# A gated cross-attention block on one core: the first fetch of x, the late weights and the weight rounding moved

## The chip, the cores and the metric

The kernel runs on one core of a Trainium2 chip. The metric is the device time of one execution in microseconds (us). The engines are TensorE (PE; PEld is its weight load), VectorE (DVE), ScalarE (ACT), GpSimd (POOL) and SyncE (SP, which here only issues DMAs).

## The reference

Sixteen sequences x of 224 tokens by 512 attend to contexts of 750 keys by 384 with 8 heads; a mask drops some keys of each sequence. A feed-forward part with quantised activations and ternary weights follows. Both parts are gated and added to x:

```
x = x + tanh(g_xattn) * xattn(layernorm(x), context, mask)
x = x + tanh(g_ffn)   * ffn(layernorm(x))

xattn: softmax(mask(q k^T / 8)) v W_o + b_o,  q = x W_q, k = context W_k, v = context W_v
ffn:   bitlinear(gelu(bitlinear(h, w1, b1)), w2, b2)
bitlinear(h, w, b): h is rms-normalised and quantised to 8 bits by row;
                    scale = 1 / max(mean|w|, 1e-5); w = clip(round(w * scale), -1, 1) / scale
```

w1 is 2048 by 512, w2 is 512 by 2048. All inputs and the output are float32, except the mask.

## The kernel before, in words

**Opening.** `order_batches` (L30) reads the mask, counts the keys that each sequence keeps, and sorts the sequences by that count into 16 slots. The first 8 slots hold up to 192 keys and the others up to 128. It leaves tables in SBUF: `sh.slots` (per slot its number of keys and its sequence), `sh.upto` (running counts of kept keys) and `sh.token` (row numbers of x). At its end `n_odd` goes to every engine's register (L150), and the program branches (L226): `compact_path` (L709) if all slots fit, which is what runs here, otherwise `dense_path`.

**Start of the compact path.** POOL first writes two ramps, `place` and `place_f` (L785 to L790), scales the sequence numbers to row offsets (`first`, L792) and zeroes two buffers `v_rest` (L851). Then:

- `fetch(i)` (L915) gathers two 128-token tiles of x by indirect DMA, which POOL issues. Three buffers of two tiles rotate.
- `select(s)` (L797) makes the list of kept keys of slot s. Six compares on DVE make `ind` (L803), PE sums it (L810), DVE makes `keys` (L819) and the mask (L826).
- `gather(s)` (L831) fetches the kept rows of the context by indirect DMA.
- `norm(i)` (L921) is the layernorm of x. DVE takes the statistics (L929, L930). POOL makes the power -1/2 (L761) and subtracts and multiplies (L938).
- `query_pieces` (L963) turns x on PE (L951) and multiplies by W_q (L972). `context_pieces` (L854) turns the context (L867) and makes keys (L876) and values (L891).

**Slots.** `scores` (L1001) makes the logits on PE (L1011), the row maxima on DVE (L1025), the exponentials on ACT (L1035), the reciprocal on DVE (L1044) and the product on POOL (L1045). `turn_probs` transposes the result (L1065, L1072) and `weighted` multiplies it by the values (L1089, L1100). While slot s runs, the context and queries of slot s+1 and the statistics of s+2 are prepared.

**Weights.** `load_weights` (L1299) loads w1 or w2 in eight blocks of 512 KB through SP. `sum_weights` (L1314) adds up magnitudes, even blocks on DVE (L1321), odd ones on ACT (L1325). `scale_weights` (L1329) makes the total over partitions with a matmul (L1333) and the scale on DVE (L1335 to L1344). `round_weights` (L1350) scales, clips and casts a block on DVE (L1354, L1355, L1356) into one of two rotating buffers `w16` with tag `xq`. `turn_weights` (L1359) transposes that on PE (L1367, L1371) and an evictor writes it as 8-bit floats. w1 is prepared within slot 0 and w2 within slot 1. `late_loads` (L220) fetches b_o, b2, W_o and b1; POOL scales b_o and b2 by the gates (L1454, L1455).

**Feed-forward part.** From slot 2 on, pairs of 128-token tiles go through `residual` (fetches of y, L1139, and the addition of b_o, L1141), `project` (L1143), `normalise` (L1172), `up` (L1209), `gelu` (L1231) and `down` (L1260). `normalise` uses two buffers with tag `xq`: `xq`, and `xqT`, a DMA transpose of it (L1196).

**What sets the order.** The lists at L1418 to L1482 are merged by hand-given costs (`merge`, L1389), which gives the order in which the program is written. A scheduler below then orders each engine's instructions by readiness and priority, so that the order on an engine is not the order of the source. [...] `evict` (L738) chooses DVE or ACT for PSUM evictions by a running balance of estimated loads.

Of the kernel before, what the change touches and what calls it, by code (L numbers as in the profile page):

```python
# [16 lines left out]
EPS = 1e-5  # L17
# [12 lines left out]
def order_batches(ctx, tc, sh, mask, x, context):  # L30
# [33 lines left out]
    def spread(dst, src, first, second):  # L64
# [8 lines left out]
        second.tensor_copy(dst[32:64, :, 5:6], by4[32:64, :, 3:4])  # L73
        second.tensor_copy(dst[64:128, :, 5:6], by4[64:128, :, 3:4])

    spread(spread_no, start, nc.gpsimd, nc.gpsimd)
    nc.gpsimd.tensor_tensor(at, at, spread_no, ALU.add)
    tri = sel.tile([TJ, TJ], BF16, name="tri")
# [11 lines left out]
    kept = sel.tile([B, 1], F32, name="kept_of")  # L90
    nc.vector.tensor_reduce(kept, m8, AX.X, ALU.add)
    nc.gpsimd.tensor_copy(m, m8)

    key = sel.tile([B, 1], F32, name="key")
    nc.vector.scalar_tensor_tensor(key, kept, float(B), number, ALU.mult, ALU.add)
# [39 lines left out]
    nc.vector.tensor_reduce(odds, odd, AX.XY, ALU.add)  # L135
    n_odd = const.tile([1, 1], mybir.dt.int32, name="n_odd")
    nc.vector.tensor_copy(n_odd, odds)

    where = sel.tile([P, 4, 8], F32, name="where")
    spread(where, sh.slots[:, 1, :], nc.vector, nc.gpsimd)  # L140
# [568 lines left out]
def compact_path(ctx, tc, sh, x, context, out, late_loads):  # L709
# [53 lines left out]
    def small(name, n=2):  # L763
        return pa.tile([P, n], F32, tag=f"s{n}", name=name, bufs=24 if n == 2 else 6)
# [16 lines left out]
        )  # L781

    place = pa.tile([P, 256], BF16, name="place")  # L785
    numbers(place[:, :192], [[1, 192]], 0, 0)
    numbers(place[:, 192:], [[1, 64]], 128, 0)
    place_f = pa.tile([TQ, 320], BF16, name="place_f")
    numbers(place_f[:, :192], [[1, 192]], 0, 0)
    numbers(place_f[:, 192:], [[1, P]], 0, 0)  # L790
    first = pa.tile([P, B], F32, name="first")
    nc.gpsimd.tensor_scalar(first, sh.slots[:, 1, :], float(J), None, ALU.mult)  # L792

    live = [{} for _ in range(B + 1)]
    kctx = context.rearrange("b j c -> (b j) c")

    def select(s):  # L797

        st = live[s]
        nt = 2 if CAPS[s] > P else 1  # L800
        ind = pa.tile([TJ, NJ, 256], BF16, tag="ind", name=f"ind_{s}", bufs=1)
        for n in range(NJ):
            nc.vector.tensor_scalar(  # L803
                ind[:, n, : nt * P], place[:TJ, : nt * P], sh.upto[:, n, s : s + 1], None, ALU.is_ge
            )
# [12 lines left out]
        keys = pa.tile([P, 2], I32, tag="keys", name=f"keys_{s}", bufs=3)  # L818
        nc.vector.tensor_scalar(  # L819
            keys[:, :nt], pi[:, :nt], float(J - 1), first[:, s : s + 1], ALU.min, ALU.add  # L820
        )
# [4 lines left out]
        nc.vector.tensor_scalar(  # L826
            mb[:, :nm], place_f[:, :nm], sh.slots[:TQ, 0, s : s + 1], -FMAX, ALU.is_ge, ALU.mult
        )
        st["mask"] = mb

# [17 lines left out]
    v_rest = []  # L848
    for i in range(2):
        t = pa.tile([P, NP, 2, DH], F32, name=f"v_rest_{i}")  # L850
        nc.gpsimd.memset(t, 0.0)  # L851
        v_rest.append(t)

    def context_pieces(s):  # L854
# [66 lines left out]
    def norm(i, ks=(0, 1)):  # L921

        xp = normed[i]
        name = f"x{i}_{ks[0]}"
        part = slice(ks[0], ks[-1] + 1)
        mv = small(f"mv_{name}", 4).rearrange("p (k n) -> p k n", k=2)
        for k in ks:
            st = small(f"bs_{name}_{k}", 6)
            nc.vector.bn_stats(st, xp[:, k, :])  # L929
            nc.vector.bn_aggr(mv[:, k, :], st)  # L930
            load["v"] += 850
        rstd = small(f"rs_{name}")
        nc.gpsimd.tensor_scalar(rstd[:, part], mv[:, part, 1], 1.0, EPS, ALU.mult, ALU.add)
        pow_half(rstd[:, part])
        less = small(f"ls_{name}")
        nc.gpsimd.tensor_scalar(less[:, part], mv[:, part, 0], -1.0, 0.0, ALU.mult, ALU.add)
        for k in ks:
            nc.gpsimd.tensor_scalar(  # L938
                xp[:, k, :], xp[:, k, :], less[:, k : k + 1], rstd[:, k : k + 1], ALU.add, ALU.mult
            )  # L940

    def slot_xnT(s):
        if "xnT" not in live[s]:
# [228 lines left out]
    def normalise(i, ks=(0, 1)):  # L1172
# [126 lines left out]
    def load_weights(wi, c):  # L1299

        raws[wi, c] = raw = late["raw"].tile([P, W], F32, tag="raw", name=f"raw_{wi}_{c}", bufs=NPC)
        if wi == 0 and c == 0:

            nc.scalar.copy(raw[0:1, 0:1], live[0]["ctx"][0:1, 0, 0:1])
        if wi == 0:
            nc.sync.dma_start(
                raw.rearrange("p (a d) -> p a d", d=D),
                sh.w1_dram[c * 2 * P : (c + 1) * 2 * P, :].rearrange("(a p) d -> p a d", p=P),
            )
        else:  # L1310
            at = c % 2 * W
            nc.sync.dma_start(raw, sh.w2_dram[c // 2 * P : (c // 2 + 1) * P, at : at + W])

    def sum_weights(wi, c):  # L1314
        if c == 0:
# [34 lines left out]
    def round_weights(wi, c):  # L1350

        raw = raws.pop((wi, c))
        quantised[wi, c] = w16 = pa.tile([P, W], BF16, tag="xq", name=f"w16_{wi}_{c}", bufs=2)
        nc.vector.tensor_scalar(raw, raw, weight_scale[wi], 1.0, ALU.mult, ALU.min)  # L1354
        nc.vector.tensor_scalar(w16.bitcast(I16), raw, -1.0, None, ALU.max)  # L1355
        nc.vector.tensor_copy(w16, w16.bitcast(I16))  # L1356
        load["v"] += 1700
# [15 lines left out]
            evict(w2T[:, f : f + 8, c // 2 * P : (c // 2 + 1) * P], pt, 8 * P)  # L1373

    def weight_pieces(wi):
        p = []
        if wi == 1:
            p += [(0.0, lambda c=c: load_weights(wi, c)) for c in range(NPC)]
        p += [(0.4, lambda c=c: sum_weights(wi, c)) for c in range(NPC)]
        p += [(0.1, lambda: scale_weights(wi))]  # L1380
        for c in range(NPC + 1):
            if c < NPC:
                p += [(0.0, lambda c=c: round_weights(wi, c))]
            if c > 0:
                p += [(0.6, lambda c=c: turn_weights(wi, c - 1))]
        return p


# [126 lines left out]
```

## Time and profile before

| what | value |
|---|---|
| median of 3 runs | 785.88 us (785.7 to 787.6) |
| the profiled execution's own time | 788.52 us |
| its span, first to last instruction | 786.8 us |
| mean granted PE clock | 0.971 |
| busy PE, DVE, ACT, POOL | 696.5, 508.5, 392.1, 367.7 us |
| first query matmul (L972) | 31.08 us |
| moved by DMA | 59.53 MB, 76 GB/s on average |

A line of a group or of the timeline gives the source line, the engine, the operation, out<-in with sizes, and how many; times are busy times, and a bracket at the end says how long the engine was idle before it and which instruction ended that. "DMA" as releaser means that the data landed. In lines of stretches each engine has its busy time and, in brackets, its instructions; the PE clock is a share of full speed. In lines of waits stand who waited for whom, the total in us, how often, and the longest. One execution is profiled, so single durations vary a little between executions.

### The profile page before, as it was taken

What the parts mean: (1) busy time and instruction counts of PE and PEld (TensorE: products, weight loads), DVE (VectorE), ACT (ScalarE), POOL (GpSimd) and SP (SyncE); (2) the same over time, 40 slices, a digit from 0 to 9 for tenths busy, and PEclk for the clock granted to TensorE, in tenths of its full rate; (3) what the DMA queues carried; (4) which work ended last, traced back from release to release, by engine and by line L of the source; (5) the groups of instructions that cost most, each with busy time, mean ns of one, the idle gap of its engine ahead of it and who ended that gap; (6) DMA issues with size and microseconds to landing.
All of it is one profiled execution on the core that took longest, in us unless ns stands there. A gap on an engine that the chain in (4) does not pass through costs nothing.

```text
span 786.8 us, 11011 instructions
## 1 busy us (share of the span) xinstructions
PE 696.5 (89%) x3790; PEld 448.0 (57%) x3790; DVE 508.5 (65%) x1281; ACT 392.1 (50%) x950; POOL 367.7 (47%) x478
## 2 busy tenths in 40 slices
PE   2588889899999899999989899989898999989762
PEld 2466666676566565665756476656574756543321
DVE  4366776667772955848568635575758577688960
ACT  0264937344563735628264674373737365455340
POOL 6834245746083451753728343655362525254331
PEclk9999999999999999999999989999999999999887
DMA  7913412101231401415032330141404031323331
GB/s 278 340 47 106 160 28 67 35 15 47 40 75 54 104 28 43 89 54 104 29 67 78 78 67 12 54 104 54 79 27 91 17 81 41 67 54 92 85 88 48
DMA packets 87280, 59.53 MB, mean 76 GB/s; under 512 B 75424, under 2 KB 75440, under 8 KB 87088
## 3 DMA queue, kind: packets, MB, share of 16 engines
q1 hardware_dynamic: 78960, 32.00, 17.6%
q0 software_dynamic: 8256, 26.75, 10.9%
q8 instruction: 32, 0.52, 0.3%
q14 instruction: 32, 0.26, 0.1%
HBM read 33.04 MB, written 7.34 MB: 51 GB/s over the span
## 4 chain that ended last, share of the span: by engine, by line
PE 63%; DVE 19%; ACT 5%; issue 4%; POOL 4%; DMA 2%; POOLq 0%; DVEq 0%; ACTq 0%; SPq 0%
PE qp L972 13%; PE fp L1264 10%; PE hp L1218 9%; PE vp L891 7%; PE kp L876 6%; PE op L1148 6%; DVE a L1241 5%; PE av L1089 3%; DVE h L1226 3%; PE ptp L1065 3%; PE sim L1011 3%; DVE hq L1244 2%; DVE ind L803 2%; PE av L1100 2%; DVE hq L1245 2%
## 5 line engine op out<-in xcount | busy, mean ns | idle before, releaser
L1045 POOL TENSOR_TENSOR p<-p,rec 112x768 f32<-112x768 f32 (+1 forms) x64 | 81.8, 1281 | 130.5 <-DVE rec L1044 61.7
L1226 DVE SCALAR_TENSOR_TENSOR h<-hp,c,b_bc 128x1024 f32<-128x1024 f32 x56 | 71.6, 1281 | 86.6 <-PE hp L1218 85.6
L1218 PE MATMUL hp<-w1T,xqT 128*128 128x512 fp8e4 x448 | 106.3, 384 | 8.9 <-DMA xqT<-xq 5.1
L1035 ACT ACTIVATE p<-p,nm 112x192 f32<-112x192 f32 (+1 forms) x256 | 106.7, 421 | 7.9 <-DVE nm L1025 7.0
L1264 PE MATMUL fp<-w2T,hqT 128*128 128x512 fp8e4 x448 | 103.7, 386 | 7.5 <-DMA hqT<-hq 7.5
L972 PE MATMUL qp<-xnT,wq_sb 128*128 128x224 f32 x512 | 106.4, 363 | 1.3 <-ACT xnT L747 1.1
L1148 PE MATMUL op<-wo_sb,xoT 128*128 128x512 f32 x224 | 106.2, 609 | 1.0 <-DVE keys L819 0.9
L972 PEld LDWEIGHTS qp<-xnT,wq_sb 128*128 128x128 f32 x512 | 98.7, 196 | 7.5 <-ACT xnT L747 1.9
L1025 DVE CUSTOM_DVE_ANT_0 p<-sim,mask 112x192 f32<-112x192 f32 (+1 forms) x256 | 70.3, 316 | 29.2 <-PE sim L1011 16.5
L1218 PEld LDWEIGHTS <-xqT 128*128 128x128 bf16 x448 | 43.8, 99 | 62.3 <-issue 13.8
L1241 DVE TENSOR_REDUCE a<-h 128x1 f32<-128x2048 f32 x28 | 63.9, 2281 | 22.6 <-ACT h L1238 22.6
L1264 PEld LDWEIGHTS <-hqT 128*128 128x128 bf16 x448 | 43.7, 99 | 59.6 <-DMA hqT<-hq 8.9
L1238 ACT ACTIVATE h<-h 128x2048 f32<-128x2048 f32 x28 | 53.5, 1912 | 42.2 <-DVE h L1226 24.4
L876 PE MATMUL kp<-ctxT,wk_sb 128*128 128x192 f32 (+1 forms) x384 | 65.5, 323 | 5.6 <-ACT xnT L747 3.6
L774 POOL DMA_INDIRECT x<-in_x_dram,token x28 | 33.1, 1182 | 77.2 <-PE ctxp L867 36.8
L891 PE MATMUL vp<-wv_sb,ctxT 128*128 128x512 f32 x144 | 68.0, 610 | 0.0
L876 PEld LDWEIGHTS kp<-ctxT,wk_sb 128*128 128x128 f32 x384 | 59.8, 207 | 13.3 <-ACT xnT L747 5.2
L747 ACT COPY qT<-qp 128x448 f32<-128x448 f32 x30 | 16.0, 532 | 94.8 <-PE qp L972 94.8
L1148 PEld LDWEIGHTS op<-wo_sb,xoT 128*128 128x128 f32 x224 | 40.4, 192 | 39.0 <-issue 35.6
L1011 PE MATMUL sim<-kT,qT 64*112 64x192 f32 (+1 forms) x512 | 55.2, 317 | 8.4 <-DVE nm L1025 7.4
L1250 ACT ACTIVATE sq<-h 128x2048 bf16<-128x2048 f32 x28 | 53.2, 1900 | 7.6 <-DMA hqT<-hq 3.9
L1011 PEld LDWEIGHTS sim<-kT,qT 64*112 64x112 f32 x512 | 37.9, 172 | 28.2 <-DVE nm L1025 11.6
(157 smaller groups left out, 1117.9 us busy)
## 6 DMA issues: line engine op xcount, KB each, us to landing
raw<-in_L_ffn_w_dram SPq DMA_DIRECT2D x16, 512.0 KB, 4.9
wq_sb<-in_L_xattn_W_q_dram SPq DMA_DIRECT2D x1, 1024.0 KB, 5.9
wo_sb<-in_L_xattn_W_o_dram SPq DMA_DIRECT2D x1, 1024.0 KB, 7.9
b_bc<-in_L_ffn_b_dram SPq DMA_DIRECT2D x1, 1024.0 KB, 11.1
wk_sb<-in_L_xattn_W_k_dram SPq DMA_DIRECT2D x1, 768.0 KB, 7.4
wv_sb<-in_L_xattn_W_v_dram SPq DMA_DIRECT2D x1, 768.0 KB, 8.9
x<-in_x_dram,token POOLq DMA_INDIRECT x28, 5.9
y<-in_x_dram,token POOLq DMA_INDIRECT x28, 3.4
```

The lines of the kernel that those rows point to most:

```text
L876: nc.tensor.matmul(pk[:, p - p0, :], lhsT=sh.wk[:, c, p * P : (p + 1) * P], rhs=st["ctxT"][:, c, :cap], start=(c == 0), stop=(c == NC - 1),)
L891: nc.tensor.matmul(pv, lhsT=st["ctxT"][:, c, t * P : (t + 1) * P], rhs=sh.wv[:, c, :], start=(c == 0), stop=(c == NC - 1),)
L972: nc.tensor.matmul(pq[:, i, :], lhsT=sh.wq[:, d, (p + i) * P : (p + i + 1) * P], rhs=st["xnT"][:, d, :], start=(d == 0), stop=(d == ND - 1),)
L1011: nc.tensor.matmul(sim[:, j, i, :cap], lhsT=st["qT"][j * DH : (j + 1) * DH, p, q * TQ : (q + 1) * TQ], rhs=st["kT"][j * DH : (j + 1) * DH, ...
L1025: nc.vector.tensor_tensor_reduce(out=probs[:, h, :cap], in0=sim[:, j, i, :cap], in1=st["mask"][:, j * begin : j * begin + cap], scale=-(DH ...
L1035: nc.scalar.activation(probs[:, h, :cap], probs[:, h, :cap], AF.Exp, bias=nmax, scale=-1.0, accum_out=total[:TQ, h : h + 1],)
L1045: nc.gpsimd.tensor_tensor(probs[:, :, :cap], probs[:, :, :cap], rec[:TQ].unsqueeze(2).to_broadcast([TQ, 4, cap]), ALU.mult,)
L1148: nc.tensor.matmul(po, lhsT=xoT[:, d, at : at + P], rhs=sh.wo[:, d, :], start=(d == 0), stop=(d == ND - 1))
L1218: nc.tensor.matmul(ph[:, n, :], lhsT=f["xqT"][:, k * ND + d, :], rhs=w1T[:, d, at : at + NB], start=(d == 0), stop=(d == ND - 1),)
L1226: nc.vector.scalar_tensor_tensor(h[:, cols], ph.rearrange("t i n -> t (i n)"), f["c1", k], sh.b1[:, cols], ALU.mult, ALU.add)
L1241: nc.vector.tensor_reduce(amax[:, k : k + 1], h, AX.X, ALU.max, apply_absolute_value=True)
L1264: nc.tensor.matmul(po, lhsT=f["hqT", k][:, n, :], rhs=w2T[:, n, :], start=(n == 0), stop=(n == NF - 1))
```

## The change

1. The two ramps become `sh.place` and `sh.place_f`, made by POOL in `order_batches`, ahead of the branch. `first` becomes `sh.first`, made by ACT ahead of the branch. `v_rest` is zeroed on DVE.
2. `norm_first(k)` replaces `norm(0, (k,))` for the first two tiles of x: epsilon is added on DVE, POOL makes the power, and DVE subtracts the mean and multiplies.
3. The other fetches and the gather of slot 1 get `tc.issue_after(norm_first(1))`: they stand in POOL's queue behind the power of the second tile. Blocks 1 to 7 of w1 stand in SP's queue behind block 0, which waits for the first context tile to land, as before.
4. w1 is summed and scaled ahead of slot 0. Four one-element copies on ACT write the sum's last column into the destinations of the late loads, so those loads wait for it.
5. In slot 0 each w1 block is rounded and then turned two blocks later. As a block is rounded, the same w2 block is loaded into the buffer that comes free, and w2 is summed in slot 0 too. In slot 1 w2's scale comes first, then rounding and turning in the same way. The tag `xq` has three buffers.

In the built program, PE's order is the same as before from the scores of slot 2 on, and that of the other engines within about a slot after that.

```diff
+    sh.place = const.tile([P, 256], BF16, name="place")
+    sh.place_f = const.tile([P, 320], BF16, name="place_f")
     spread(spread_no, start, nc.gpsimd, nc.gpsimd)
...
     nc.gpsimd.tensor_copy(m, m8)
+    numbers(sh.place[:, :192], [[1, 192]], 0, 0)
+    numbers(sh.place[:, 192:], [[1, 64]], 128, 0)
+    numbers(sh.place_f[:, :192], [[1, 192]], 0, 0)
+    numbers(sh.place_f[:, 192:], [[1, P]], 0, 0)
...
+    sh.first = const.tile([P, B], F32, name="first")
+    nc.scalar.activation(sh.first, sh.slots[:, 1, :], AF.Copy, scale=float(J))
...
-    place = pa.tile([P, 256], BF16, name="place")
-    numbers(place[:, :192], [[1, 192]], 0, 0)
-    numbers(place[:, 192:], [[1, 64]], 128, 0)
-    place_f = pa.tile([TQ, 320], BF16, name="place_f")
-    numbers(place_f[:, :192], [[1, 192]], 0, 0)
-    numbers(place_f[:, 192:], [[1, P]], 0, 0)
-    first = pa.tile([P, B], F32, name="first")
-    nc.gpsimd.tensor_scalar(first, sh.slots[:, 1, :], float(J), None, ALU.mult)
...
-        nc.gpsimd.memset(t, 0.0)
+        nc.vector.memset(t, 0.0)
...
+    def norm_first(k):
+
+        xp = normed[0]
+        st = small(f"bs_x0_{k}", 6)
+        nc.vector.bn_stats(st, xp[:, k, :])
+        mv = small(f"mv_x0_{k}", 4)
+        nc.vector.bn_aggr(mv[:, :2], st)
+        rstd = small(f"rs_x0_{k}")
+        nc.vector.tensor_scalar(rstd[:, :1], mv[:, 1:2], EPS, None, ALU.add)
+        power = nc.gpsimd.tensor_tensor(rstd[:, :1], rstd[:, :1], sh.mhalf[:, :1], ALU.pow)
+        nc.vector.tensor_scalar(xp[:, k, :], xp[:, k, :], mv[:, 0:1], rstd[:, :1], ALU.subtract, ALU.mult)
+        return power.ins
...
-            f["xq"] = pa.tile([P, 2, D], BF16, tag="xq", name=f"xq_{i}", bufs=2)
-            f["xqT"] = pa.tile([P, 2 * ND, P], BF16, tag="xq", name=f"xqT_{i}", bufs=2)
+            f["xq"] = pa.tile([P, 2, D], BF16, tag="xq", name=f"xq_{i}", bufs=3)
+            f["xqT"] = pa.tile([P, 2 * ND, P], BF16, tag="xq", name=f"xqT_{i}", bufs=3)
...
-        quantised[wi, c] = w16 = pa.tile([P, W], BF16, tag="xq", name=f"w16_{wi}_{c}", bufs=2)
+        quantised[wi, c] = w16 = pa.tile([P, W], BF16, tag="xq", name=f"w16_{wi}_{c}", bufs=3)
...
     def weight_pieces(wi):
+
         p = []
         if wi == 1:
-            p += [(0.0, lambda c=c: load_weights(wi, c)) for c in range(NPC)]
-        p += [(0.4, lambda c=c: sum_weights(wi, c)) for c in range(NPC)]
-        p += [(0.1, lambda: scale_weights(wi))]
-        for c in range(NPC + 1):
+            p += [(0.0, lambda: scale_weights(1))]
+        for c in range(NPC + 2):
             if c < NPC:
-                p += [(0.0, lambda c=c: round_weights(wi, c))]
-            if c > 0:
-                p += [(0.6, lambda c=c: turn_weights(wi, c - 1))]
+                p += [(0.2, lambda c=c: round_weights(wi, c))]
+                if wi == 0:
+                    p += [(0.0, lambda c=c: load_weights(1, c))]
+            if c > 1:
+                p += [(0.6, lambda c=c: turn_weights(wi, c - 2))]
+                if wi == 0:
+                    p += [(0.0, lambda c=c: sum_weights(1, c - 2))]
         return p
...
     fetch(0)
     select(0)
     gather(0)
-    norm(0, (0,))
-    norm(0, (1,))
-    fetch(1)
     select(1)
-    gather(1)
+    norm_first(0)
+    with tc.issue_after(norm_first(1)):
+        fetch(1)
+        gather(1)
+        fetch(2)
+    late["stage"] = ExitStack()
+    late["raw"] = late["stage"].enter_context(tc.tile_pool(name="raw", bufs=1))
+    with tc.issue_after(load_weights(0, 0)):
+        for c in range(1, NPC):
+            load_weights(0, c)
     for piece in query_pieces(0) + context_pieces(0):
         piece[1]()
-    fetch(2)
     for _, piece in norm_pieces(1):
         piece()
     select(2)
-    late["stage"] = ExitStack()
-    late["raw"] = late["stage"].enter_context(tc.tile_pool(name="raw", bufs=1))
     for c in range(NPC):
-        load_weights(0, c)
+        sum_weights(0, c)
+    scale_weights(0)
+
+    for dst in (sh.wo[0:1, 0, 0:1], sh.bo[0:1, 0:1], sh.b1[0:1, 0:1], sh.b2[0:1, 0:1]):
+        nc.scalar.copy(dst, weight_sums[0][0:1, NPC - 1 : NPC])
     late_loads()
```

`tc.issue_after(ins)` gives each instruction that is recorded inside the block, on the engine of `ins`, an ordering edge to `ins`: it is queued behind it on that engine. `load_weights` returns its DMA instruction for this; the uses of `place`, `place_f` and `first` take the new names.

More of the change, by code (lines that the diff above doesn't have):

```diff
@@ L803, in select @@
             nc.vector.tensor_scalar(
-                ind[:, n, : nt * P], place[:TJ, : nt * P], sh.upto[:, n, s : s + 1], None, ALU.is_ge
+                ind[:, n, : nt * P], sh.place[:TJ, : nt * P], sh.upto[:, n, s : s + 1], None, ALU.is_ge
             )
@@ L819, in select @@
         nc.vector.tensor_scalar(
-            keys[:, :nt], pi[:, :nt], float(J - 1), first[:, s : s + 1], ALU.min, ALU.add
+            keys[:, :nt], pi[:, :nt], float(J - 1), sh.first[:, s : s + 1], ALU.min, ALU.add
         )
@@ L826, in select @@
         nc.vector.tensor_scalar(
-            mb[:, :nm], place_f[:, :nm], sh.slots[:TQ, 0, s : s + 1], -FMAX, ALU.is_ge, ALU.mult
+            mb[:, :nm], sh.place_f[:TQ, :nm], sh.slots[:TQ, 0, s : s + 1], -FMAX, ALU.is_ge, ALU.mult
         )
@@ L1305, in load_weights @@
         if wi == 0:
-            nc.sync.dma_start(
+            return nc.sync.dma_start(
                 raw.rearrange("p (a d) -> p a d", d=D),
                 sh.w1_dram[c * 2 * P : (c + 1) * 2 * P, :].rearrange("(a p) d -> p a d", p=P),
[L1309 to L1312, printed above, removed]
+            ).ins
+        at = c % 2 * W
+        return nc.sync.dma_start(raw, sh.w2_dram[c // 2 * P : (c // 2 + 1) * P, at : at + W]).ins
     def sum_weights(wi, c):
```

## The prediction

> **What bounds the kernel now.** I read the engines' shares first, then busy time by stretches, the timeline of the opening, and the waits. TensorE (PE) is busy 89% of the span:
>
> ```profile
> span 786.8 us, 11011 instructions
> PE 696.5 (89%) x3790; PEld 448.0 (57%) x3790; DVE 508.5 (65%) x1281; ACT 392.1 (50%) x950; POOL 367.7 (47%) x478
> ```
>
> What can be gained is PE's idle time. The built program has the same order on PE from slot 2's scores on, and on the other engines within a slot of that, so I cut the first 146 us at PE's landmarks (columns: stretch, length, busy PE, PEld, DVE, ACT, POOL, PE clock, DMA share, GB/s):
>
> ```profile
> 0.00:26.70 26.70, 4.87 (x42) 3.97 (x42) 12.38 (x46) 2.15 (x5) 17.55 (x50) 1.00 0.80 276
> 49.69:60.48 10.79, 7.79 (x71) 6.36 (x68) 8.07 (x44) 8.31 (x32) 8.15 (x7) 1.00 0.35 92
> 60.48:91.18 30.70, 26.87 (x181) 21.04 (x181) 23.48 (x56) 18.71 (x46) 8.05 (x9) 0.94 0.43 143
> 91.18:107.80 16.62, 15.27 (x114) 12.63 (x113) 9.48 (x47) 11.44 (x36) 11.14 (x12) 1.00 0.23 68
> 107.80:129.64 21.84, 18.95 (x131) 13.13 (x129) 16.17 (x35) 11.75 (x25) 3.66 (x4) 0.92 0.03 5
> 129.64:146.00 16.36, 12.82 (x73) 10.20 (x72) 9.27 (x21) 6.31 (x16) 15.08 (x17) 0.90 0.29 91
> ```
>
> PE idles 3.0, 3.8, 1.35, 2.9 and 3.5 us in the last five; the opening is nearly all idle. The timeline shows what holds it:
>
> ```profile
> 12.09 1.25 POOL L774 DMA_INDIRECT x<-in_x_dram,token  x1 [0.18 <-issue]
> 20.64 0.69 DVE L929 BATCH_NORM_STATS2 bs_x<-x 128x6 f32<-128x512 f32 x1 [5.89 <-DMA x<-in_x_dram,token]
> 25.94 0.77 POOL L938 TENSOR_SCALAR x<-x,ls_x,rs_x 128x512 f32<-128x512 f32 x1
> 31.08 7.97 PE L972 MATMUL qp<-xnT,wq_sb 128*128 128x224 f32 x32 [0.57 <-ACT xnT L747]
> ```
>
> x is issued at 12.09 behind POOL's setup and lands 8.55 us later, behind four late weights (2.5 MB, issued at 9.58 to 11.0). Its centring on POOL waits behind gathers and ends at 26.7. In slots 0 and 1 PE waits for DVE's rounding or POOL's products:
>
> ```profile
> PE wp L1367 <- DVE w L1356: 2.2, 1, 2.2
> PE ptp L1065 <- POOL p L1045: 1.8, 1, 1.8
> PE wp L1371 <- DVE w L1356: 2.7, 2, 1.7
> PE ptp L1065 <- DVE y L1151: 3.5, 1, 3.5
> ```
>
> [...] six selection compares take 1.30 us alone, 2.48 beside a 1.47 us product.
>
> ```profile
> 12.13 1.30 DVE L803 TENSOR_SCALAR ind<-place,upto 125x256 bf16<-125x256 bf16 x6
> 53.87 2.48 DVE L803 TENSOR_SCALAR ind<-place,upto 125x256 bf16<-125x256 bf16 x6
> ```
>
> [...] the clock is 0.50 at 62 to 64 us, and twelve key matmuls take 3.80 us there, 2.13 elsewhere.
>
> ```profile
> 61.78 3.80 PE L876 MATMUL kp<-ctxT,wk_sb 128*128 128x192 f32 x12
> 100.98 2.13 PE L876 MATMUL kp<-ctxT,wk_sb 128*128 128x192 f32 x12
> ```
>
> [...] x took 5.6 to 7.3 us from issue beside w1, y has a median of 3.4.
>
> **The start.** Moved ahead of the branch: four iotas (1.0 us of POOL between 4.9 and 6.1, where it waited; free unless they delay the permutation at 6.14, then 0.2), and the scaling of the batch offsets, onto ACT (idle, 0.2, free). POOL is free at 9.4, so x issues at 9.4 and 10.95 (pitch 1.55 as before). With no late weights ahead I take 4.0 us to landing (bounds 3.4 and 6.4). DVE now has two memsets first. No such row exists[...]. Then DVE in the built order: memsets to 10.5, six compares 1.4, mask 0.4, keys 0.2, six compares 1.3: 13.8. Statistics 0.69, keys and aggregate 0.4, the second tile's statistics 0.69, epsilon 0.15: 15.7. Power on POOL 0.58, centring on DVE 0.4 (half of a 1024-column 0.66, and hand-over): 16.7. Second tile, epsilon, power and centring again: 17.9. Five hand-overs, 0.5; from there to the first query matmul 1.7 (29.39 to 31.08): 20.1 against 31.08. **Gain 11.0** (10 to 11.5).
>
> **A new wait at the keys.** POOL issues eight transfers from 17.5 on, 1.30 apart: the last starts at 26.6 and lands at 29.9 to 33.0 (3.3 to 6.4 us later). The built order has DVE do that tile's statistics, behind a weight sum of 1.21, before it evicts the second half of the context's transposes, which ACT did before. The key matmuls wait for that. PE gets there at 20.1 + 8.0 + 0.8 = 28.9; the eviction ends at 31.7 to 34.8. I take 33.5: a wait of 4.6 (2.8 to 5.9). Before, keys began at 40.16. **6.7 of the lead are left.** w1 starts at about 16, when the first context tile lands; 4 MB plus the fetches at the 390 GB/s of 34 to 36 us are in by about 34, before PE reaches its sum at 43.
>
> **Slot 0.** The order now puts the first turn of w1 ahead of the second x transposes and the keys. On DVE stand behind the first scores: eight maxima at 0.28, the reciprocal after four exponentials at 0.44, four compares, and scale, clip and cast (0.66, 0.60, 0.34): the turn comes 6.9 us after the scores, PE has 4.1 us to do, so it idles 2.8; POOL's scaling of b_o and b2 (1.57, 1.58) and its product collide and may add 2. b_o's hold is hidden: issued at about 41.7 when w1 is summed, it lands at about 47, when POOL has done its gathers; if it came later, the product behind it would wait as long. I take 3.8 against 3.0 before: **-0.8** (+0.5 to -2.5). In the rest of slot 0, with turns two blocks behind, DVE has about 18 us of work to PE's 24: its 3.8 us of waits go, **+3.8** (2 to 3.8). On ACT the four one-element copies that release the late loads (0.2 each) come before the first exponentials, where it is idle; on SP the late loads now stand between w1 and w2, whose own buffers come free later still. The 3 buffers cost no time. w2's loads and sums move up into this slack.
>
> **Slot 1.** Here scale_weights stands at the head. After the first scores DVE does eight maxima with the reciprocal (to 3.0 us), keys, two compares and four maxima (4.8), reciprocal, aggregates and four compares (6.2), total, mean and reciprocals (7.3), then scale, clip, the next scale, cast: 9.6 us. PE has 3.7 us to do before that turn, and transposes and keys stand behind it. Idle 5.9; two products and one x normalisation (4.5 us of POOL) may add half of that. I take 7.0 against 1.35: **-5.7** (-4 to -7.5). The later 2.9 us go: **+2.9** (1.5 to 2.9).
>
> **Clock.** Before has two half-clock spells in these slots, 1.7 us each. [...] **0** (-3.4 to +3.4).
>
> **Slot 2's opening.** POOL's y fetches wait for the last clip of w2; POOL then adds b_o in front of a product, and DVE's compares (5 in 5.56 us) and PE (3.5 us, and 1.7 for the clock) wait. Rounding may now run one block further ahead of PE, so this starts some 8 us earlier relative to PE. Half of it: **+2.5** (0 to 5.2). Beyond it the order stays; xqT's third buffer I count at nothing (one 5.1 us wait for xqT could shrink).
>
> **Sum**: 6.7 - 0.8 + 3.8 - 5.7 + 2.9 + 0 + 2.5 = 9.4 us. The profiled execution took 788.52 (span 786.8), and would take 779.1; the runs' median is 785.88, so 776.5.
>
> **Rivals.** (A) The fetches land early and no turn holds PE: the waits of 4.6 and 7.0 shrink to 3 and 4, the clock gives 2 and slot 2 gives 5: about 769. For it: a gather with nothing beside it landed in 3.2 us; against: DVE's order is fixed, and the chains above are counted in it. (B) A wash: the keys' wait is 6, the turns 5 and 8, a third spell, nothing from slot 2: gain about 1.5, 784.4. (C) Slower: DVE becomes the bound of slots 0 and 1, because sixteen turns stand in PE's queue amid attention[...]. Fourteen turns follow each slot's first; past (9.4 + 2.4) / 14 = 0.84 us of wait at each it is slower; at 1.2 each it loses 16.8 and ends at 793. For it: one clip took 1.95 us beside a product; against: DVE is busy 57 of the 80 us from 49.69 to 129.64. The change not doing what it says is excluded for the opening, since the built order shows the fetch first.
>
> **Numbers.** Forecast (gain 4 to 13) 0.60, A 0.18, B 0.14, C 0.08. What a measurement of this kernel can tell from no change is about 0.3%, 2.4 us: faster 0.82, within it 0.10, slower 0.08. The range of 768 to 785 takes in most of A and B and leaves out C.
>
> **What would show it.** Right: first query matmul at about 20, an idle PE before the keys that ends with DVE's ctxT eviction behind x's landing, first scores at about 43, an idle of 6 us or more before slot 1's first turn, slot 2 some 7 us earlier. Wrong: scores much before 40 (A), PE waiting for DVE's cast at most turns (C), or w1 landing after 41, which would hold PE at the sum.

## The result, and the profile after

The changed kernel takes 782.02 us (median of 7 runs, 781.12 to 784.07) beside 786.64 us for the kernel before on the same chip (7 runs): a ratio of 0.9938, with a 95% interval of 0.9926 to 0.9950. That is 4.9 us faster, where 9.4 us were forecast. The profiled execution took 783.66 us (span 781.9).

The shares of the engines hardly move:

```profile
span 781.9 us, 11017 instructions
PE 699.3 (89%) x3790; PEld 453.5 (58%) x3790; DVE 514.0 (66%) x1292; ACT 391.4 (50%) x950; POOL 369.5 (47%) x469
```

The timeline of the opening answers to the four lines shown of before. x is issued at 10.51 in place of 12.09, lands 3.8 us later in place of 8.55, is centred on DVE in 0.55 us, and the first query matmul starts at 20.77 in place of 31.08:

```profile
10.51 1.49 POOL L784 DMA_INDIRECT x<-in_x_dram,token  x1 [1.86 <-DVE v_rest L851]
14.35 0.69 DVE L946 BATCH_NORM_STATS2 bs_x<-x 128x6 f32<-128x512 f32 x1 [0.49 <-DMA x<-in_x_dram,token]
17.15 0.55 DVE L952 TENSOR_SCALAR x<-x,mv_x,rs_x 128x512 f32<-128x512 f32 x1 [0.42 <-POOL rs_x L951]
20.77 8.72 PE L985 MATMUL qp<-xnT,wq_sb 128*128 128x224 f32 x32 [0.57 <-ACT xnT L757]
```

Then it stops. Of these ten microseconds 0.9 are left at the first scores (48.79 against 49.69). The timeline shows a wait at the keys, for an eviction that stands on DVE behind the statistics of two x tiles and a sum of w1. The last of these tiles was issued at 27.81 and landed 7.2 us later, at 35.05:

```profile
27.81 1.01 POOL L784 DMA_INDIRECT x<-in_x_dram,token  x1 [0.30 <-issue]
33.98 0.69 DVE L929 BATCH_NORM_STATS2 bs_x<-x 128x6 f32<-128x512 f32 x1 [0.52 <-DMA x<-in_x_dram,token]
34.59 1.20 DVE L1333 TENSOR_REDUCE wsums<-raw 128x1 f32<-128x1024 f32 x1
35.71 0.68 DVE L929 BATCH_NORM_STATS2 bs_x<-x 128x6 f32<-128x512 f32 x1
36.31 0.41 DVE L754 COPY ctxT<-ctxp 128x256 f32<-128x256 f32 x1
36.77 6.44 PE L876 MATMUL kp<-ctxT,wk_sb 128*128 128x192 f32 x20 [5.25 <-DVE ctxT L754]
```

Before, the keys waited only 0.5 us, and all 24 of them ran at full clock (1.00):

```profile
40.16 4.17 PE L876 MATMUL kp<-ctxT,wk_sb 128*128 128x192 f32 x24 [0.46 <-ACT ctxT L747]
```

The cut by stretches (start:end, length, then busy time of PE, PEld, DVE, ACT and POOL, PE's clock, DMA share, GB/s) says what else was paid. The keys themselves ran at half clock (0.52). PE idles 3.8 us at the start of slot 0 (48.79 to 64.18) and 7.3 us at the start of slot 1 (86.67 to 101.80), which has half the clock again in its second half (0.50 from 93.9 to 104.2 us). The rest of both slots has almost no idle time, and slot 2's opening only 0.4 us:

```profile
36.77:43.04 6.27, 6.27 (x20) 6.27 (x21) 2.75 (x3) 0.37 (x1) 0.00 (x0) 0.52 0.00 0
48.79:64.18 15.39, 11.63 (x93) 9.70 (x93) 14.68 (x45) 8.94 (x27) 12.39 (x8) 0.89 0.80 286
64.18:86.67 22.49, 22.32 (x146) 17.31 (x147) 19.55 (x46) 17.25 (x42) 9.30 (x9) 1.00 0.48 161
86.67:101.80 15.13, 7.81 (x71) 6.42 (x69) 13.47 (x50) 8.92 (x30) 8.74 (x9) 0.74 0.04 14
101.80:127.60 25.80, 25.80 (x173) 21.30 (x172) 14.77 (x33) 13.89 (x30) 14.81 (x12) 0.95 0.27 73
127.60:140.00 12.40, 12.03 (x82) 9.52 (x81) 7.73 (x33) 6.87 (x22) 10.72 (x13) 1.00 0.11 36
```

PE's waits between 14 and 150 us (engine and line that waited, for whom, total, times, longest) name them. The wait of before for y is gone, and those for rounded weights fell from 4.9 us in all to 3.3. The first transposes of x wait 3.5 us for DVE's chain, where the kernel before had them wait for GpSimd's. New are the waits for the keys' operand, for the sum of w2 in slot 1 and, behind it, for w2's first rounded block:

```profile
PE kp L876 <- DVE ctxT L754: 5.3, 1, 5.3
PE wtotp L1345 <- DVE wtot L1343: 4.2, 1, 4.2
PE xnp L964 <- DVE rs_x L950: 3.5, 1, 3.5
PE wp L1383 <- DVE w L1368: 2.5, 1, 2.5
PE ptp L1078 <- POOL p L1058: 2.5, 2, 2.1
```

The lead over the kernel before, read at the same landmarks of both traces, beside the forecast's running sum:

| landmark | forecast lead | measured lead |
|---|---|---|
| first query matmul (31.08, now 20.77) | 11.0 | 10.3 |
| first scores (49.69, now 48.79) | 6.7 | 0.9 |
| slot 1's first two groups of scores done (92.09, now 88.23) | 9.7 | 3.9 |
| slot 2's first two groups done (130.55, now 129.16) | 6.9 | 1.4 |
| slot 2's first query matmul (142.99, now 137.10) | 9.4 | 5.9 |
| slot 3's first scores (147.04, now 140.81) | 9.4 | 6.2 |
| end of the span (786.8, now 781.9) | 9.4 | 4.9 |

So slots 0 and 1 in sum give and cost what was forecast (+3.0 for 3.0, -2.5 for -2.8). The loss beyond the forecast is in one stretch, the 28 us from the first query matmul to the first scores: 9.4 us of lead go there, where 4.3 were forecast. A larger gain at slot 2 makes up for part of it (4.5 for 2.5), and near 404 us another 1.3 us go.

### The profile page after: what moved, and what is told of

The parts are those of the page before. It is cut to its first block, busy times and chain, and to the rows that moved or that the text cites. A ratio compares the mean times of both kernels' runs of the same rounds, so it can differ in the third digit from the quotient of the medians.

```text
span 781.9 us, 11017 instructions
## 1 busy us (share of the span) xinstructions
PE 699.3 (89%) x3790; PEld 453.5 (58%) x3790; DVE 514.0 (66%) x1292; ACT 391.4 (50%) x950; POOL 369.5 (47%) x469
## 4 chain that ended last, share of the span: by engine, by line
PE 61%; DVE 21%; ACT 6%; issue 4%; DMA 4%; POOL 2%; DVEq 0%; POOLq 0%; ACTq 0%; SPq 0%
PE qp L985 11%; PE fp L1277 10%; PE hp L1231 9%; PE kp L876 7%; PE vp L891 6%; PE op L1161 5%; DVE a L1254 5%; PE av L1102 3%; PE ptp L1078 3%; DVE h L1239 3%; PE sim L1024 3%; DVE hq L1257 2%; DVE p L1038 2%; DVE hq L1258 2%; PE av L1113 2%
## 5 line engine op out<-in xcount | busy, mean ns | idle before, releaser
L876 PE MATMUL kp<-ctxT,wk_sb 128*128 128x192 f32 (+1 forms) x384 | 69.2, 336 | 10.2 <-DVE ctxT L754 5.3
L876 PEld LDWEIGHTS kp<-ctxT,wk_sb 128*128 128x128 f32 x384 | 64.0, 219 | 18.3 <-ACT xnT L757 5.7
L891 PE MATMUL vp<-wv_sb,ctxT 128*128 128x512 f32 x144 | 66.3, 597 | 0.0
L1024 PE MATMUL sim<-kT,qT 64*112 64x192 f32 (+1 forms) x512 | 53.6, 315 | 8.9 <-DVE nm L1038 8.7
```

The source lines that it names most:

```text
L876: nc.tensor.matmul(pk[:, p - p0, :], lhsT=sh.wk[:, c, p * P : (p + 1) * P], rhs=st["ctxT"][:, c, :cap], start=(c == 0), stop=(c == NC - 1),)
L891: nc.tensor.matmul(pv, lhsT=st["ctxT"][:, c, t * P : (t + 1) * P], rhs=sh.wv[:, c, :], start=(c == 0), stop=(c == NC - 1),)
L1024: nc.tensor.matmul(sim[:, j, i, :cap], lhsT=st["qT"][j * DH : (j + 1) * DH, p, q * TQ : (q + 1) * TQ], rhs=st["kT"][j * DH : (j + 1) * DH, ...
```

## The experiments

My theory after this reading: the early start is lost to one wait (the keys) and to the half clock after it, and slot 1's head and slot 2's opening are one exchange. The rivals: that the start is worth little because the slots are bound by VectorE anyway, or that the new order of the weights gives back what the start gains. Ratios below are to the kernel before on the same chip, with 95% intervals; "span" is that of the profiled execution. The moment at which the branch is reached differs between profiled executions: the copy of "upto" ahead of it starts at 8.1 to 8.2 us in some and at 8.9 to 9.1 in others (8.86 in the kernel before, 9.09 in the changed one). Where two traces of different starts are compared, the difference is taken off, and it is said.

**The start alone, and the weights alone.** The first puts the handling of w1 and w2 and the plain issue of the late loads back; the second puts back the fetches, the centring on GpSimd, and the setup behind the branch.

```diff
 (e1_start_only)
-    with tc.issue_after(load_weights(0, 0)):
-        for c in range(1, NPC):
-            load_weights(0, c)
...
-    for dst in (sh.wo[0:1, 0, 0:1], sh.bo[0:1, 0:1], sh.b1[0:1, 0:1], sh.b2[0:1, 0:1]):
-        nc.scalar.copy(dst, weight_sums[0][0:1, NPC - 1 : NPC])
+    for c in range(NPC):
+        load_weights(0, c)
     late_loads()
 (e2_weights_only)
-    norm_first(0)
-    with tc.issue_after(norm_first(1)):
-        fetch(1)
-        gather(1)
-        fetch(2)
+    norm(0, (0,))
+    norm(0, (1,))
+    fetch(1)
```

> Only the start of the change: x is fetched first, its first two tiles are centred on VectorE, the other fetches are held; w1 is loaded, summed, rounded and turned as in the kernel before. Theory (the gain of the start is lost again to the wait at the first keys and to the half clock after it): first query matmul at 21, a wait of about 5 us before the keys at 36 to 37, keys at half clock, first scores only about 1 us earlier than the 49.7 us of the kernel before; from there the weights are handled as before, so 785 us (783 to 787). Rival (the start is what gains, and the new handling of the weights gives half of it back): 777 us.

Measured: 789.37 us, ratio 1.0017 (1.0006 to 1.0029), slightly slower than before. The wait at the keys is there (7.7 us), but the first query matmul came at 26.17 and not at 21, and neither the theory's 785 us nor the rival's 777 came. With wo, b_o, b1 and b2 issued at 8.9 to 10.3 again, x landed 9.6 us after its issue:

```profile
9.58 1.50 POOL L784 DMA_INDIRECT x<-in_x_dram,token  x1 [1.86 <-DVE v_rest L851]
19.20 0.69 DVE L946 BATCH_NORM_STATS2 bs_x<-x 128x6 f32<-128x512 f32 x1 [6.27 <-DMA x<-in_x_dram,token]
```

> Only the handling of the weights (w1 summed ahead of the scores, late loads held behind it, rounding two blocks ahead of turning, w2 loaded and summed in slot 0), with the start of the kernel before. Here the eviction of ctxT stands on ScalarE and nothing holds the first keys. Theory: the waits in slot 0 shrink by 3 us net, slot 1 pays 6 of wait and 2.5 of half clock, the opening of slot 2 gains 4.5, later slot 0 and 1 waits go for 2.9: 784 us (781 to 786), so the weights and not the start bring what the whole change brings. Rival (start gains, weights lose): 788 to 790.

Measured: 783.88 us, ratio 0.9953 (0.9936 to 0.9970), as the theory has it. Counted from that copy the first scores come only 0.5 us later than in the changed kernel (48.26 with the copy at 8.10, 48.79 with it at 9.09), without any of the new fetching: nothing holds the keys there, and x lands 3.6 us after its issue, since the late loads are held here too. By the two ratios three quarters of the whole gain come without the fast start. That is not yet the fast start's worth, since in the changed kernel it is lost at the keys.

**The hold of the late loads.** One run takes it out of the changed kernel, the other puts one into the kernel before; there the late loads wait for the first context rows and for their turn behind w1's loads, not for w1's sum.

```diff
 (e8_no_hold, changed kernel)
-    for dst in (sh.wo[0:1, 0, 0:1], sh.bo[0:1, 0:1], sh.b1[0:1, 0:1], sh.b2[0:1, 0:1]):
-        nc.scalar.copy(dst, weight_sums[0][0:1, NPC - 1 : NPC])
 (e9_before_hold, kernel before)
-    for c in range(NPC):
-        load_weights(0, c)
+    with tc.issue_after(load_weights(0, 0)):
+        for c in range(1, NPC):
+            load_weights(0, c)
+    for dst in (sh.wo[0:1, 0, 0:1], sh.bo[0:1, 0:1], sh.b1[0:1, 0:1], sh.b2[0:1, 0:1]):
+        nc.scalar.copy(dst, live[0]["ctx"][0:1, 0, 0:1])
     late_loads()
```

> The changed kernel without the four copies that hold wo, b_o, b1 and b2 behind the sum of w1; they are issued at about 9 to 10 us again. Theory (what brings x early is that nothing else moves then): x lands 9 us after its issue in place of 4, first query matmul at 25 to 26, first scores at 53 to 54, and the 2 us of waiting for a late b_o in slot 0 go: 785.5 us (784 to 787). Rival (the start counts for little, the weights for all): 782.

Measured: 791.10 us, ratio 1.0036 (1.0015 to 1.0057): slower than the kernel before, and by the two ratios some 8 us over the changed one. x lands 9.6 us after its issue, the first scores come at 55.39. These four one-element copies decide the sign of the whole change:

```profile
8.90 0.33 SPq L231 DMA_DIRECT2D bo_bc<-in_L_xattn_b_o_dram  x1
9.60 1.51 POOL L784 DMA_INDIRECT x<-in_x_dram,token  x1 [1.87 <-DVE v_rest L851]
9.81 0.38 SPq L233 DMA_DIRECT2D wo_sb<-in_L_xattn_W_o_dram  x1
12.54 1.79 POOL L1474 TENSOR_SCALAR bo_bc<-bo_bc,tgates 128x512 f32<-128x512 f32 x1
19.15 0.69 DVE L946 BATCH_NORM_STATS2 bs_x<-x 128x6 f32<-128x512 f32 x1 [6.18 <-DMA x<-in_x_dram,token]
```

The 785.5 us of the theory were too low: it counted the hold only as x landing in 4.0 us, and the removed hold also brings GpSimd's scaling of b_o between its first gathers.

> The kernel before, in which wo, b_o, b1 and b2 are held until the first context rows have landed and are queued behind w1; fetches, centring on GpSimd and the weights' order stay as they were. Theory (the late loads in front of x are the largest part of what the change mends at the start): x lands about 4 us after its issue in place of 8.5, first query matmul at 27 to 28.5 in place of 31.1, first scores at 46 to 47, and most of that lead comes through slots whose waits are as before: 784 us (782.5 to 785.5) where the kernel before has 787. Rival (the hold pays only together with the new order of the weights, because a late b_o stops GpSimd or the lead runs into slot 0's rounding): 786 to 788.

Measured: 786.07 us, ratio 0.9977 (0.9963 to 0.9990). x does land 3.7 us after its issue (12.07, 15.74), but the first query matmul comes only 1.9 us earlier (29.17), because the centring on GpSimd still ends at 24.8 for the first tile: PE waits 11.0 us for it. So the theory's time was missed, and the rival's range holds the time for another reason than it gave. By the ratios a hold alone gives 1.8 us, the rest of the fast start without it (e1) loses 1.3, and in the changed kernel, beside the fast start, the hold is worth some 8 (e8): the two need each other.

**The wait and the clock at the keys.** The first run takes the wait away by moving one eviction to ScalarE; the second leaves the wait and fills it.

```diff
 (e3_evict_act)
-            evict(st["ctxT"][:, c0:c1, : nt * P], pt, (c1 - c0) * nt * P)
+            cols = (c1 - c0) * nt * P
+            if s == 0 and c0 == 2:
+                load["v"] += 80 + 1.2 * cols
+                nc.scalar.copy(st["ctxT"][:, c0:c1, : nt * P], pt)
+            else:
+                evict(st["ctxT"][:, c0:c1, : nt * P], pt, cols)
 (e4_warm_keys)
+            if s == 0 and c0 == 2:
+                idle = wide([P, S], F32, "idle")
+                for n in range(18):
+                    nc.tensor.matmul(idle, lhsT=sh.wq[:, n % ND, :P], rhs=st["xnT"][:, n % ND, :], start=True, stop=True)
```

> The changed kernel, with the second eviction of slot 0's ctxT on ScalarE instead of VectorE, where it stood behind the statistics of later x. Theory: the wait of 5.3 us before the keys goes, and with it the half clock of the keys (2.8 us); first scores at 41 to 42; of these 7 to 8 us some 1 to 2 are lost to the sum of w1 and the late loads being late: 776 us (774 to 778). Rival (the lead is taken back in slot 0, whose weight blocks and late loads come no earlier): 781 to 782.

Measured: 779.49 us, ratio 0.9890 (0.9864 to 0.9916). The first scores come at 40.81, 8.0 us before the changed kernel's, so the wait and the half clock together were worth that. By the ratios 3.8 us reach the end, in the two profiled executions 2.8: neither the theory's 776 us nor the rival's 781 to 782. The timeline of slot 0 shows where the rest stays: with everything 8 us earlier, b_o is issued at 41.28 and has not landed when GpSimd wants it, and the product of the second scores stands behind its scaling, that of b2 and two gathers.

```profile
47.66 2.53 POOL L1481 TENSOR_SCALAR bo_bc<-bo_bc,tgates 128x512 f32<-128x512 f32 x1 [2.82 <-DMA bo_bc<-in_L_xattn_b_o_dram]
50.18 1.88 POOL L1063 TENSOR_TENSOR p<-p,rec 112x768 f32<-112x768 f32 x1
52.05 2.32 POOL L1482 TENSOR_SCALAR b_bc<-b_bc,tgates 128x512 f32<-128x512 f32 x1
57.07 1.47 POOL L1063 TENSOR_TENSOR p<-p,rec 112x768 f32<-112x768 f32 x1
58.59 1.01 PE L1083 MATMUL ptp<-ident,p 112*128 112x112 f32 x4 [4.89 <-POOL p L1063]
```

> The changed kernel, with 18 query matmuls more on TensorE, into a PSUM tile that nobody reads, while it waits for ctxT before the first keys (about 4.5 of the 5.3 us). The wait itself stays. Theory (the idle gap is what brings the half clock): the first 24 key matmuls take about 4.3 us in place of 7, first scores near 46 us, 779.5 us (778.5 to 780.5). Rival (the half clock comes from something else, a load on the chip or the time since the start): keys as slow as before, 782 us.

Measured: 782.01 us, ratio 0.9929 (0.9906 to 0.9952), which at the end can't be told from the changed kernel's 0.9938: the time is the rival's. The trace decides for the theory's mechanism: the keys start at the same 36.8, run at full clock, and the first scores come at 46.61 in place of 48.79.

```profile
29.98 6.97 PE L873 MATMUL idle<-xnT,wq_sb 128*128 128x224 f32 x36
36.79 4.23 PE L880 MATMUL kp<-ctxT,wk_sb 128*128 128x192 f32 x24
```

From 36.77 to 43.04 us the clock is 1.00 here and 0.52 in the changed kernel. The idle gap, then, brought the half clock at the keys, and it cost 2.2 us. These were eaten in slot 0, where PE waited 2.8 us for selection compares on DVE (four took 2.75 us there; six took 1.25 at 10.77 us in the changed kernel). In this run the late loads were also issued 8 us earlier than in the changed kernel (b_o at 38.98 for 46.97), so its end alone would not measure the clock.

**GpSimd's order in slot 0.** The scaling of b_o and b2 is ordered behind slot 0's last product, with the eviction on ScalarE (e6) and with the late start of the weights-only run (e12); the two differ by the fast start alone.

```diff
-                nc.gpsimd.tensor_scalar(sh.bo, sh.bo, sh.tgates[:, 0:1], None, ALU.mult)
-                nc.gpsimd.tensor_scalar(sh.b2, sh.b2, sh.tgates[:, 1:2], None, ALU.mult)
+                with tc.issue_after(live[0]["divided"]):
+                    nc.gpsimd.tensor_scalar(sh.bo, sh.bo, sh.tgates[:, 0:1], None, ALU.mult)
+                    nc.gpsimd.tensor_scalar(sh.b2, sh.b2, sh.tgates[:, 1:2], None, ALU.mult)
```

("divided" is the slot's last product with the reciprocal, kept when it is written.)

> As the run with the eviction of ctxT on ScalarE, and GpSimd's scaling of b_o and b2 ordered behind slot 0's last product instead of ahead of its third. Theory (the 5.4 us in which TensorE waited for a product there were those of a late load): the wait falls under 1.5 us, and 3 to 4 us more of the earlier start come through: 775.5 us (774 to 777.5). Rival (VectorE's rounding of w1 is as late as the product, and takes its place): 778.5 to 780.

Measured: 776.11 us, ratio 0.9853 (0.9837 to 0.9869). PE's 5.4 us of waiting for a product become 0.6. With 0.9 us taken off for its earlier branch, the first scores lead the changed kernel's by 7.9 us, slot 3's by 7.0, and the span's end by 6.9. From the changed kernel to this one the intervals are far apart, while the step from e3 to e6 alone just overlaps (0.9864 and 0.9869); the trace shows that step. The chain is wait at the keys, half clock, then a late b_o.

> The run with the new weights alone (start of the kernel before, late loads held) with GpSimd's scaling of b_o and b2 ordered behind slot 0's last product. Beside the run with ctxT on ScalarE and the same order (776.1 us), which differs from it by the fast start alone. Theory (the fast start is worth what it brings the first scores forward by, 8 us, once nothing takes it back): 783 us (781.5 to 784.5). Rival (most of the 776 came from the order on GpSimd): 778 to 780.

Measured: 781.49 us, ratio 0.9925 (0.9899 to 0.9951). By the ratios the fast start is thus worth about 5.7 us once nothing takes it back (0.9925 against 0.9853), less than the theory's 8; in the changed kernel it is worth 1.2 (0.9953 against 0.9938), less than the intervals.

**Slot 1 and slot 2.** An empty piece delays w2's scaling in slot 1 of the changed kernel (e5) and of e6 (e7); e10 also orders GpSimd's additions of b_o behind slot 2's first two products.

```diff
 (e5_slot1_lead, e7_all)
-            p += [(0.0, lambda: scale_weights(1))]
+            p += [(1.5, lambda: None), (0.0, lambda: scale_weights(1))]
 (e10_all_y: as e7_all, and)
-        for k in range(2):
-            nc.gpsimd.tensor_tensor(y[:, k, :], y[:, k, :], sh.bo, ALU.add)
+        if i == 0:
+            late["divided"] = live[2]["divided"]
+        with tc.issue_after(late["divided"]):
+            for k in range(2):
+                nc.gpsimd.tensor_tensor(y[:, k, :], y[:, k, :], sh.bo, ALU.add)
```

> The changed kernel, with an empty piece of cost 1.5 ahead of the scaling of w2 in slot 1, so that on TensorE six key matmuls of the next slot and slot 1's later scores stand ahead of the sum of w2, and the keys ahead of its first turn. Theory (the waits of 4.2 and 2.5 us there and the half clock after them are lost time): slot 1 shortens by 4 to 7 us, of which some is taken by VectorE's later work: 778 us (776 to 780) where the changed kernel has 782. Rival (VectorE is the bound of slot 1, so the waits only move to later turns): 781.5 to 783.

Measured: 782.02 us, ratio 0.9929 (0.9906 to 0.9952): no difference from the changed kernel, as the rival said. Both waits of slot 1 are gone, and slot 2's scores follow slot 1's after 38.6 us in place of 40.9. The loss is behind that, in slot 2, whose first query matmul comes 14.4 us after its scores in place of 9.5. Its profiled execution was the longest of its six (787.85 us), so the next run shows it better.

> The three edits together: ctxT's eviction on ScalarE, the scaling of b_o and b2 later, and the empty piece in slot 1. Theory (the waits are separate, and what each gives adds up): 771.5 us (769 to 774). Rival (slots 0 and 1 are bound by VectorE, so one gain is taken from the other): no better than the better of the two single ones.

Measured: 778.16 us, ratio 0.9877 (0.9858 to 0.9896), no better than e6 alone (the intervals overlap); the gains don't add up. Counted from the branch, slot 2's scores stand 4.1 us before e6's, and its first query matmul 0.5 us behind. GpSimd and PE in slot 2:

```profile
109.26 1.18 POOL L784 DMA_INDIRECT y<-in_x_dram,token  x1 [7.10 <-DVE w L1372]
124.12 1.26 POOL L1159 TENSOR_TENSOR y<-y,bo_bc 128x512 f32<-128x512 f32 x1 [1.03 <-DMA y<-in_x_dram,token]
125.34 2.89 POOL L1063 TENSOR_TENSOR p<-p,rec 112x768 f32<-112x768 f32 x2
126.86 0.45 PE L1083 MATMUL ptp<-ident,p 112*128 112x112 f32 x1 [3.28 <-POOL p L1063]
```

y's fetches wait for DVE's last clip of w2, six of them with the additions of b_o take GpSimd 16 us, and the products that PE needs stand behind. Counted from the branch this chain ends only 1.3 us earlier than in e6, where PE comes 4.1 us later and finds it done.

> As the run with the three edits together, and GpSimd's additions of b_o to the first three y ordered behind slot 2's first two products. Theory (delaying w2 in slot 1 moved these additions into the path of slot 2's products, which is where the 3 us that slot 1 gave went): the 5.5 us of waiting for a product in slot 2 fall to about 1, slot 2's first query matmul comes 10 us after its scores in place of 14: 773 us (771.5 to 775). Rival (the products wait for VectorE's rounding of w2 and not for the additions): 777 to 779, as without the edit.

Measured: 774.53 us, ratio 0.9836 (0.9808 to 0.9864), inside the forecast, and by the ratios 3.2 us under e7, with intervals that just touch (0.9864 and 0.9858). The wait of 3.3 us for a product in slot 2 is gone, so the additions were what that product waited for. Of the 5.5 us that the expectation named, the other 2.2 lay in slot 1 and stayed. Slot 2's first query matmul comes 11.0 us after its scores in place of 14.2. Against e6 the intervals overlap (0.9808 to 0.9864 and 0.9837 to 0.9869).

**The first issue.** The clearing of v_rest moves behind the centring.

```diff
 (e11_all_y_zero, in norm_first)
+        if k == 1:
+            with tc.issue_after(centre.ins):
+                for t in v_rest:
+                    nc.vector.memset(t, 0.0)
```

> As the run before it, and the two clearings of v_rest on VectorE ordered behind the centring of the second tile instead of first behind the branch. Theory (GpSimd's first issue came 1.1 us later than forecast because VectorE's clearing held it up): x is issued at 9.5 to 9.8 in place of 10.5, first query matmul about 1 us earlier, end 0.5 to 1 us earlier than the run before it. Rival (GpSimd's first issue takes that long after the branch anyway): x issued at 10.4, no difference.

Measured: 773.85 us, ratio 0.9831 (0.9804 to 0.9857), not told apart from e10. x is issued 1.41 us after the copy of "upto" starts, with the clearing in front or not, as the rival had it; only the issue itself is shorter, 1.22 us in place of 1.49, and x lands 0.3 us earlier.

```profile
8.09 0.24 ACT L133 COPY upto<-pc 125x96 f32<-125x96 f32 x1 [0.79 <-PE pc L131]
9.50 1.22 POOL L784 DMA_INDIRECT x<-in_x_dram,token  x1 [1.86 <-DVE ind L803]
13.14 0.69 DVE L950 BATCH_NORM_STATS2 bs_x<-x 128x6 f32<-128x512 f32 x1 [1.35 <-DMA x<-in_x_dram,token]
```

This version and e10 are the fastest measured: 1.6 to 1.7% under the kernel before, against 0.6% for the change as it stands.

## Why the prediction was wrong about the size

The direction held, and the range holds the time, but the gain was forecast about twice too large. At one step 5.8 us less of the lead were left than forecast. That slot 2 gave 2.0 us more than forecast is luck, and hides a part of this. By the forecast's own steps:

- **The start, 11.0 us.** Measured 10.3. x was issued at 10.51 and not at 9.4; its landing (3.8 us for 4.0) and DVE's chain were right. DVE's clearing took 1.03 us for 1.1, a figure that rested on no trace (GpSimd's two clearings had taken 0.63 us each before), and did not cause the late issue (e11).
- **"6.7 of the lead are left."** This step failed; measured 0.9. The mechanism was right, the eviction behind the last tile's statistics and a sum of w1, but two terms were wrong. The first, 3.3 us, is the landing of the last x tile. The eviction ended at 36.7 and not at 33.5, beyond the upper bound of 34.8. Of this, 1.2 us come from the tile's later issue (27.81 for 26.6) and the rest from its landing: 3.3 to 6.4 us were allowed and 7.2 measured. The four transfers that were issued before w1's loads (17.18) landed after 3.0 to 3.8 us, the eight after them took 6.4 to 7.6. The prediction had itself read 5.6 to 7.3 us beside w1 in the trace of before, and then allowed less. The second term, 2.5 us, was put at nothing: the keys ran at half clock, so that from keys to scores it took 12.0 us in place of 9.5. The forecast named the wait, and didn't ask what the same idle gap does to the clock of the work behind it. e4 shows that half clock: 20 key matmuls took 6.44 us behind the gap of 5.3 us, and 24 took 4.23 with the gap filled. e3 shows wait and clock together as 8.0 us.
- **Slot 0, -0.8 and +3.8.** Measured +3.0 in sum for 3.0. "b_o's hold is hidden" came out nearly right (GpSimd waited 0.6 us for it), but only since the scores were late. Had the lead of 6.7 been there, b_o would have been late: in e3 GpSimd waits 2.8 us for it and PE 4.9 us for the product behind. A lead of 6.7 at the scores would hardly have been a gain of 9.4 at the end either: in e3 the lead there is 8.9, and the gain by the ratio 8.7. I had written that the product would wait as long if b_o came later; I hadn't joined that with my own earlier scores.
- **Slot 1, -5.7 and +2.9.** Measured 7.3 us of idle for 7.0, no later waits, -2.5 in sum for -2.8.
- **Clock, 0.** This was an estimate of mine, from two spells in the trace of before. Spells at 36 to 43, 56 to 60 and 94 to 104 us for the two of before: at the keys alone -2.5. Within the slots the sums came out as forecast all the same; what made up for the longer spell of slot 1 was not taken apart. At 404 us another 1.3 is lost (below).
- **Slot 2's opening, +2.5.** Measured +4.5. The mechanism was as forecast: y's fetches start 9.9 us before the slot's second scores, against 2.4 before, 7.5 earlier where 8 was said. Taking half of it was wrong: 3.2 of the 3.5 us of waiting went, and with it the half clock that followed before, from 140.3 to 143.7 us. What slot 1 pays and what slot 2 gains have one cause, rounding w2 early, as e5 and e7 show from the other side.

Of the rivals, B (a wash, 784.4) came nearer to the time than the forecast, and named the right places, a wait of 6 at the keys and a third spell; what it left out is slot 2. C, slower because DVE binds, is excluded: DVE is busy 20 us of the 22.5 from 64 to 87, yet PE is idle only 0.2.

What stays open: what fills the 1.4 us between the copy of "upto" and x's issue. No run moved w1's loads behind the gathers of x, so what their late landing alone costs is not measured. That DVE's chain through w2 is what bounds slots 1 and 2 in e7 was read from its trace, and shown only for its last link, the additions.

## What to carry to other kernels

A forecast of a start that comes earlier must be carried on to each resource that is released by time and not by that start: here the last fetch, then b_o, then y, and each took the lead in turn until it was moved. Take a transfer's landing time from transfers that ran beside the same load (here 3.0 to 3.8 us ahead of w1's loads, 6.4 to 7.6 beside them). Price an idle gap on TensorE as the gap and a possible half clock behind it (here 5.3 us and, by e4, 2.2). When a wait is moved out of one slot, look for what stood behind it on the third engine; here three unrelated small operations (two scalings, an addition), which stood ahead of products on GpSimd, became waits of TensorE (4.9 us in e3, 3.3 in e7).

## What the runs showed that I had not expected

The same wait of 2.1 us before a transpose of x, near 404 us, is followed by half clock in eight of the fourteen profiled kernels and not in the other six. In the changed kernel twelve key matmuls then take 2.75 us, in the kernel before 1.50:

```profile
404.48 1.09 PE L964 MATMUL xnp<-ident,x 128*128 128x128 f32 x4 [2.14 <-ACT xnT L757]
405.37 2.75 PE L876 MATMUL kp<-ctxT,wk_sb 128*128 128x128 f32 x12
```

```profile
410.65 0.66 PE L951 MATMUL xnp<-ident,x 128*128 128x128 f32 x4 [2.15 <-ACT xnT L747]
411.14 1.50 PE L876 MATMUL kp<-ctxT,wk_sb 128*128 128x128 f32 x12
```

The granted clock itself shows what decides it. In each of the fourteen traces every change of the clock lies on one grid of 3.41 us: in the changed kernel the spells start at 35.9, 56.4, 93.9 and 404.5 us, which are 6, 11 and 91 steps apart, and they last 6.8, 3.4, 10.2 and 3.4 us. Where the grid lies, counted from the start of the program, differs from trace to trace. In the changed kernel the wait (402.34 to 404.48) falls into one step, in which PE is busy 1.27 us of 3.41, and the next step has half clock:

```profile
401.13:404.54 3.41, 1.27 (x8) 0.67 (x7) 3.41 (x10) 3.38 (x11) 0.00 (x0) 1.00 0.44 84
404.54:407.96 3.42, 3.42 (x16) 3.30 (x16) 3.41 (x14) 2.79 (x7) 1.81 (x2) 0.50 0.44 82
```

In the kernel before a border of the grid cuts the same wait (408.51 to 410.65), no step is that empty, and the clock stays:

```profile
406.50:409.91 3.41, 2.01 (x15) 1.10 (x11) 3.41 (x5) 3.38 (x7) 0.00 (x0) 1.00 0.18 36
409.91:413.33 3.42, 2.62 (x24) 2.30 (x24) 3.42 (x17) 3.23 (x8) 1.65 (x1) 1.00 0.63 117
```

In the eight kernels with the half clock PE was busy 37 to 39% of the step in which the wait began, in the six others 44 to 70%. From about 31 us on, over all fourteen traces, each of the 90 full-clock steps with PE busy for less than 41.5% was followed by a step at half clock, and of the 2701 steps with more than 54.5% only five were; in between it was 34 of 62. So it is the place of the wait on the grid that counts here. Nothing in the kernels is seen to set it, so I take it for chance. It moves the end by 1.3 us, a quarter of what the change gained, so a difference of that size between two single traces says little.

GpSimd's scaling of b_o took 1.57 us in the kernel before, at 31.06 with nothing on DVE, and 2.53 in slot 0 of the changed kernel, at 53.38 with DVE busy for 2.09 us of it, mostly with a block's scale, clip and cast.
